# The input projection of groups 2 to 4 moved into the first scan, with the gate's matmul reading x contiguously

## Chip, cores and metric

The kernel runs on one core of a Trainium2 chip. The metric is device time in microseconds (us) of one execution; the figure before is the median of three runs. A profile of one further execution shows every engine: TensorE (PE, with its weight loads PEld), VectorE (DVE), ScalarE (ACT), GpSimd (POOL) and SyncE (SP, which issues most DMAs).

## The reference

Input x is 32 sequences of 256 tokens of 256 features, all float32. The result is x plus an FFN block applied to a conditioning block:

```
x + ffn(cond(x, cond_2048))

cond:  xr, gate = split(x @ W_in.T)            # 256 -> 2 x 512
       xr  = silu(causal conv of 4 taps (xr + cond_2048))
       xn  = layernorm(xr)
       B, C, dt = split(xn @ W_xproj.T)        # 16 states each
       h_t = clip(h_(t-1) * a_t + b_t x xn_t, -10, 10)     # 256 steps
       y_t = C_t . h_t + D * xn_t
       out = (y * silu(gate)) @ W_out.T
ffn:   two layers of local attention (8 heads, windows of 128)
       and a gated feed-forward (hidden 682), each with a residual
```

## The kernel before

The sequences are taken in four groups of eight (GB = 8). For each group there is a scan (the conditioning block) and a main part (two layers of attention and feed-forward, `blocks`). The scan of group 1 (`g == 0` in the code, `alone`) runs by itself at the start. Then the main part of each group is issued with the scan of the next group beside it: `side_by_side` takes the pieces of both generators in proportion, so each engine's queue has the two interleaved. The main part of group 4 has no scan beside it.

A scan puts 16 states by 8 sequences on the 128 partitions and the 512 inner features along the free dimension. It goes in chunks of 32 tokens (CH), eight per group, and is written as an agenda: `at(s, what, ...)` puts a piece of work at step s, and step s of the recurrence is also piece s. With s0 the first step of a chunk, the parts that matter here are:

- `load_x` (line 340) at s0 - 43: SP issues two DMAs of 128 KB into `xg` (two buffers).
- `project` (line 322): one block of 128 output rows of the input projection, two matmuls of 128 x 256 that accumulate, each of which the profile shows as two records. The four conv blocks stand at s0 - 40, -38, -36 and -34, the four gate blocks at s0 + 13, 16, 17 and 18. The gate blocks read x with its tokens in another order, since the gate is needed in the order in which the scan's results are laid out:

```
if ch >= NC_:
    x = x.rearrange("p b (i q) -> p q i b", q=NQ)
```

- `conv_in` (line 351), `conv_taps`, `conv_out` take a conv block out of its PSUM bank, and lead to the normalised `xn`, which is written to memory as `xnd` (line 462) and read back spread over the states as `xrep` (line 547; three buffers of two tokens each).
- `scale_row` (line 564, ACT) scales a row, `step` (line 570, DVE; profile line 573) is the recurrence, `read_out` (line 580, PE; line 585) forms y from four steps at a time with four matmuls.
- `gate_th` (line 617, ACT) and `gate_out` (line 622, DVE) turn a gate block into `sg`, one and two steps after its projection.
- `raw_sums` (line 393), `norm_turn` (line 418), `figures` (line 474), `out_turn` (line 634) and `project_y` (line 658) are the scan's other matmuls.

In the first scan, half of the rows are spread by PE instead of DMA (`spread_rows`, line 549, into `bx`, from `xq`, which `load_skip` loads into the `rot` buffers). PSUM is one pool of eight banks with one tag, `w`, for everything. Each engine works through its own queue in the order in which the program was built.

## Time and profile before

| | us |
|---|---|
| median of three runs | 4182.01 (4180.69 to 4185.67) |
| the profiled execution | 4183.47 |
| its span, first to last instruction | 4181.7 |
| mean granted TensorE clock | 0.966 of full |
| first scan, step 0 to step 255 | 70.7 to 462.8 |
| last additions of groups 1, 2, 3, 4 | 1502.3, 2492.6, 3486.8, 4175.4 |

The profile's page gives busy time of each engine over the span, then in 40 equal slices. Views by stage give, for a stretch of time, its length and each engine's busy time with the number of records, then the granted PE clock, the share of time in which the DMA engines were busy, and GB/s. Lists in order of time give the start, the time that the merged run of records takes, the engine, the line, what is written from what, and, in brackets, the idle time before it and who ended it. Lists of groups give after the bar the busy time, the mean ns of one record, and the idle time ahead of it with who ended most of it. Matmuls overlap in the pipeline and their ends are modelled, so a matmul's own time is longer than the time from its start to the next one's start.

### The profile page before, as it was taken

To read this page: it belongs to the slowest core of one execution; us is meant where nothing else is said; L and a number is where in the kernel's file an instruction comes from. 1 tells how busy PE (TensorE), PEld (TensorE's weight loads), DVE (VectorE), ACT (ScalarE), POOL (GpSimd) and SP (SyncE) were. 2 spreads that over 40 slices of the span, in tenths; PEclk is the share of its full clock that TensorE was granted. 3 is DMA by queue.
4 is the path that set the end of the run, shared out by engine and by line. 5 is a ranking of instruction groups with operands and counts; after the bars stand their busy time and mean duration, and the time that the engine had idled before them with its cause. 6 is when DMAs were issued, how large, how long until landed. Compare 5 with 4: busy or idle time off the path is not lost. (4 is left out here: it accounts for less than half of the span.)

```text
span 4181.7 us, 51837 instructions
## 1 busy us (share of the span) xinstructions
PE 3874.3 (93%) x18236; PEld 2002.1 (48%) x18236; DVE 2619.7 (63%) x4986; ACT 1742.8 (42%) x3217; POOL 1708.1 (41%) x1749
## 2 busy tenths in 40 slices
PE   6999899899988999899998999989998899999999
PEld 3333355444544455444455445544454545654653
DVE  5888467677766456766867636776776644434443
ACT  2555344444444334444544424444444533322331
POOL 3443265225543156423654136522454315513531
PEclk9999899999999999999999999999999999999999
DMA  3444213444335212344434421344433521000000
GB/s 123 121 124 119 58 44 95 113 117 112 91 87 139 81 43 77 111 110 111 116 86 114 121 65 44 81 126 111 118 91 84 142 78 37 3 19 22 1 11 31
DMA packets 257345, 353.09 MB, mean 84 GB/s; under 512 B 160867, under 2 KB 170420, under 8 KB 254900
## 3 DMA queue, kind: packets, MB, share of 16 engines
q1 hardware_dynamic: 172624, 337.67, 29.0%
q10 hardware_dynamic: 84452, 12.01, 1.8%
q8 instruction: 147, 2.41, 0.2%
q14 instruction: 122, 1.00, 0.1%
HBM read 314.49 MB, written 33.55 MB: 83 GB/s over the span
## 5 line engine op out<-in xcount | busy, mean ns | idle before, releaser
L573 DVE CUSTOM_DVE_ANT_0 h<-h,xrep,lim 128x512 f32<-128x512 f32 x1024 | 908.1, 887 | 94.8 <-PE y L585 36.0
L566 ACT ACTIVATE xrep<-xrep,beta 128x512 f32<-128x512 f32 x896 | 608.6, 716 | 793.3 <-DMA xrep<-xnd 732.8
L781 PE MATMUL ps_qkv<-wqkv_sb,res 128*128 128x512 f32 x1536 | 740.5, 621 | 28.4 <-ACT qT L825 6.6
L805 POOL TENSOR_TENSOR rot<-rot,swp 128x512 f32<-128x512 f32 x256 | 329.2, 1286 | 653.3 <-DVE swp L802 603.3
L781 PEld LDWEIGHTS ps_qkv<-wqkv_sb,res 128*128 128x128 f32 x1536 | 286.6, 196 | 381.9 <-issue 309.0
L813 POOL TENSOR_TENSOR rn<-ss,neg_half 128x8 f32<-128x8 f32 x256 | 437.4, 1708 | 21.6 <-DVE ss L811 9.7
L797 DVE TENSOR_TENSOR rot<-ps_qkv,rc_sb 128x512 f32<-128x512 f32 x256 | 175.6, 686 | 375.6 <-ACT sq L794 375.4
L330 PE MATMUL ps_in<-xg,w_in_sb 128*128 128x256 f32 x1024 | 398.4, 523 | 6.5 <-ACT pT L995 3.4
L1140 PE MATMUL po_f<-ag,w_sb 128*128 128x512 f32 (+1 forms) x768 | 356.0, 612 | 18.5 <-DVE ag L1121 18.5
L585 PE MATMUL y<-h,ly 128*32 128x512 f32 x2048 | 354.0, 639 | 11.3 <-DVE h L573 10.1
L1111 PE MATMUL pa<-hT,w_sb 128*128 128x512 f32 (+1 forms) x896 | 363.0, 595 | 0.0
L1121 DVE SCALAR_TENSOR_TENSOR ag<-pa,b_sb,gl 128x512 f32<-128x512 f32 x192 | 143.5, 747 | 317.9 <-PE pa L1111 166.2
L1111 PE MATMUL pg<-hT,w_sb 128*128 128x512 f32 x640 | 309.4, 606 | 0.0
L330 PEld LDWEIGHTS ps_in<-xg,w_in_sb 128*128 128x128 f32 x1024 | 194.1, 204 | 206.5 <-issue 125.2
L814 POOL TENSOR_TENSOR rot<-rot,rn 128x512 f32<-128x512 f32 x256 | 280.3, 1095 | 19.0
L377 DVE SCALAR_TENSOR_TENSOR acc<-xr,wc_sb,acc 128x256 f32<-128x256 f32 x384 | 199.2, 523 | 116.7 <-POOL acc L366 114.2
L1074 POOL TENSOR_TENSOR rstd<-ve,neg_half 128x1 f32<-128x1 f32 x128 | 75.8, 592 | 476.6 <-DVE ve L1072 466.1
L995 ACT ACTIVATE pT<-sc 128x512 f32<-128x512 f32 x384 | 206.3, 592 | 127.3 <-PE sc L986 113.7
L831 PE MATMUL ps_wo<-oT,wo_sb 128*128 128x256 f32 x1024 | 237.3, 385 | 0.0
L1140 PEld LDWEIGHTS po_f<-ag,w_sb 128*128 128x128 f32 (+1 forms) x768 | 135.1, 190 | 203.3 <-issue 138.7
L794 ACT ACTIVATE sq<-ps_qkv 128x512 f32<-128x512 f32 x256 | 148.8, 593 | 195.9 <-PE ps_qkv L781 148.1
L1111 PEld LDWEIGHTS pa<-hT,w_sb 128*128 128x128 f32 (+1 forms) x896 | 135.6, 170 | 189.3 <-issue 175.7
(151 smaller groups left out, 5592.9 us busy)
## 6 DMA issues: line engine op xcount, KB each, us to landing
xrep<-xnd SPq DMA_DIRECT2D x448, 512.0 KB
xnd<-xn SPq DMA_DIRECT2D x64, 256.0 KB
wqkv_sb<-in_wqkv_dram SPq DMA_DIRECT2D x8, 1536.0 KB
xd<-xnd SPq DMA_DIRECT2D x192, 64.0 KB
w_sb<-in_w_dram SPq DMA_DIRECT2D x8, 1364.0 KB
xg<-in_xT_dram SPq DMA_DIRECT2D x64, 128.0 KB
ys<-yo ACTq DMA_DIRECT2D x64, 128.0 KB
res<-ys SPq DMA_DIRECT2D x32, 256.0 KB
```

What stands on the lines that cost most here:

```text
L330: nc.tensor.matmul(ps, w_in_sb[:, k, ch * P : (ch + 1) * P], x, start=(k == 0), stop=(k == KM - 1),)
L566: nc.scalar.activation(bx, ck[c].pop(("bx", t), bx), AF.Copy, scale=ck[c]["beta"][:, t : t + 1])
L573: nc.vector._custom_dve(TENSOR_ADD_SAT, out=h_new, in0=state["h"], in1=bx, s0=ck[c]["lim"][:, 0, t : t + 1], s1=ck[c]["lim"][:, 1, t : t + 1],
L585: nc.tensor.matmul(ck[c]["y", hb][32 * q : 32 * q + 32, :], ly[hb % 2][:, 32 * t : 32 * t + 32], ck[c].pop(("h", hb * TB + t)), start=(i = ...
L781: nc.tensor.matmul(ps, res[b // 2][:, k, b % 2, t0 : t0 + W], wqkv_sb[:, k, a * DI : (a + 1) * DI], start=(k == 0), stop=(k == KM - 1),)
L805: nc.gpsimd.tensor_add(rot, rot, swp)
L813: nc.gpsimd.tensor_tensor(rn, ss, neg_half, ALU.pow)
L814: nc.gpsimd.tensor_mul(rot, rot, bc(rn, 2, DH))
L831: nc.tensor.matmul(po[:, d], wo_sb[:, c, d * P : (d + 1) * P], oT[:, c, :], start=(c == 0), stop=(c == NC_ - 1),)
L995: nc.scalar.activation(p, banks[r], AF.Exp)
L1111: nc.tensor.matmul(ps[0:n, :], self.w1[:, k, half_ * HID + o : half_ * HID + o + n], self.h[j][:, k].rearrange("p b t -> p (b t)"), start= ...
L1140: nc.tensor.matmul(self.po[d], self.w2[r0 : r0 + n, m, d * P : (d + 1) * P], self.ag[m][r0 : r0 + n, :], start=(m == 0), stop=(m == len(MC ...
```

## The change

The scan of group 1 now also makes the input projection of groups 2 to 4. There are 96 units, each of two blocks (r = 0, 1) of one chunk of one group: 3 groups x 8 chunks x 4 pairs. For unit u, due at step s = -36 + u * 284 // 96, the program adds a load of x for every fourth unit (at s - 5), four matmuls into one PSUM bank (at s), a copy by ACT to SBUF (at s + 2) and a DMA of 256 KB to a buffer in memory (at s + 5). The scans of groups 2 to 4 no longer load x or project; they load 256 KB with two finished blocks, four times per chunk, at s0 - 44, s0 - 42, s0 + 3 and s0 + 5, and the blocks are read from SBUF where they were read from PSUM.

All projections, those of group 1's own gate too, now read x contiguously. The gate's tokens are put in their other order by ACT when it copies from PSUM (`reorder`): for the 48 gate units in two halves each, and for group 1's own gate block by block into `sg`, which `gate_th` and `gate_out` then read.

The new loads of x take buffers of tag `rot`, the copies buffers of tag `pT` (six, one of them held by the spreading weights in this scan); the loads of finished blocks take the two of tag `xg`. Nothing else of the computation is changed.

```diff
+        def reorder(out, ps):
+            nc.scalar.copy(
+                out.rearrange("p (q i b) -> p b i q", q=NQ, b=GB),
+                ps.rearrange("p (b i q) -> p b i q", q=NQ, b=GB),
+            )
+
+        projected = {}
...
-            def project(c, ch):
-                ps = bank(ps_w, "w", "ps_in")[:, 0 : GB * CH]
+            def in_rows(ps, xg, ch):
                 for k in range(KM):
-                    x = ck[c]["xg"][:, k]
-                    if ch >= NC_:
-                        x = x.rearrange("p b (i q) -> p q i b", q=NQ)
                     nc.tensor.matmul(
                         ps,
                         w_in_sb[:, k, ch * P : (ch + 1) * P],
-                        x,
+                        xg[:, k],
                         start=(k == 0),
                         stop=(k == KM - 1),
                     )
+
+            def project(c, ch):
+                ps = bank(ps_w, "w", "ps_in")[:, 0 : GB * CH]
+                in_rows(ps, ck[c]["xg"], ch)
                 ck[c]["ps", ch] = ps
+
+            def ahead_load(u):
+                if u % NC_ == 0:
+                    gg, c = 1 + u // NC_ // NCH, u // NC_ % NCH
+                    t = ap_.tile([P, KM, GB, CH], FP, tag="rot", name="xa", bufs=4)
+                    for k in range(KM):
+                        nc.sync.dma_start(
+                            out=t[:, k],
+                            in_=xT[:, k, gg * GB : (gg + 1) * GB, c * CH : (c + 1) * CH],
+                        )
+                    state["xa", u // NC_] = t
+
+            def ahead_project(u):
+                ps = bank(ps_w, "w", "ps_a").rearrange("p (r n) -> p r n", r=2)
+                for r in range(2):
+                    in_rows(ps[:, r], state["xa", u // NC_], 2 * (u % NC_) + r)
+                state["pa", u] = ps
+
+            def ahead_copy(u):
+                t = aw.tile([P, 2, GB * CH], FP, tag="pT", name="xs_a", bufs=6)
+                ps = state.pop(("pa", u))
+                if u % NC_ < NC_ // 2:
+                    nc.scalar.copy(t, ps)
+                else:
+                    for r in range(2):
+                        reorder(t[:, r], ps[:, r])
+                state["ta", u] = t
+
+            def ahead_put(u):
+                d = dp.tile([P, 2, GB * CH], FP, tag=f"ahead{u}", name=f"ahead{u}", bufs=1)
+                nc.sync.dma_start(out=d, in_=state.pop(("ta", u)))
+                projected[u] = d
+
+            def load_projected(c, i):
+                t = sp.tile([P, 2, GB * CH], FP, tag="xg", name="xp", bufs=2)
+                nc.sync.dma_start(out=t, in_=projected[((g - 1) * NCH + c) * NC_ + i])
+                for r in range(2):
+                    ck[c]["ps", 2 * i + r] = t[:, r]
...
             def gate_th(c, ch):
-                th = sp.tile([P, GB * CH], FP, tag="th", name="th_g", bufs=2)
-                nc.scalar.activation(th, ck[c]["ps", NC_ + ch], AF.Tanh, scale=0.5)
-                ck[c]["th"] = th
-
-            def gate_out(c, ch):
                 if ch == 0:
                     ck[c]["sg"] = sp.tile([P, NC_, GB * CH], FP, tag="sg", name="sg")
+                ps = ck[c].pop(("ps", NC_ + ch))
+                if alone:
+                    reorder(ck[c]["sg"][:, ch], ps)
+                    ps = ck[c]["sg"][:, ch]
+                th = sp.tile([P, GB * CH], FP, tag="th", name="th_g", bufs=2)
+                nc.scalar.activation(th, ps, AF.Tanh, scale=0.5)
+                ck[c]["th"] = th, ps
+
+            def gate_out(c, ch):
+                th, ps = ck[c].pop("th")
                 nc.vector.scalar_tensor_tensor(
-                    ck[c]["sg"][:, ch], ck[c].pop("th"), 1.0, ck[c].pop(("ps", NC_ + ch)),
-                    ALU.add, ALU.mult,
+                    ck[c]["sg"][:, ch], th, 1.0, ps, ALU.add, ALU.mult
                 )
...
-                at(s0 - 43, load_x, c)
-                for ch in range(NC_):
-                    at(s0 - 40 + 2 * ch, project, c, ch)
-                for ch, s in enumerate((13, 16, 17, 18)):
-                    at(s0 + s, project, c, NC_ + ch)
+                if alone:
+                    at(s0 - 43, load_x, c)
+                    for ch in range(NC_):
+                        at(s0 - 40 + 2 * ch, project, c, ch)
+                    for ch, s in enumerate((13, 16, 17, 18)):
+                        at(s0 + s, project, c, NC_ + ch)
+                else:
+                    for i, s in enumerate((-44, -42, 3, 5)):
+                        at(s0 + s, load_projected, c, i)
...
+            if alone:
+                n = (NG - 1) * NCH * NC_
+                for u in range(n):
+                    s = -36 + u * (NCH * CH + 28) // n
+                    at(s - 5, ahead_load, u)
+                    at(s, ahead_project, u)
+                    at(s + 2, ahead_copy, u)
+                    at(s + 5, ahead_put, u)
```

## The prediction

> **What bounds the kernel now.** I read the totals first, then stages. On the page, in the engine rows and the 40 slices, TensorE (PE) is the only engine near full:

> ```profile
> PE 3874.3 (93%) x18236; PEld 2002.1 (48%) x18236; DVE 2619.7 (63%) x4986; ACT 1742.8 (42%) x3217; POOL 1708.1 (41%) x1749
> ...
> PE   6999899899988999899998999989998899999999
> ```

> The starts of the recurrence steps (line 573) and the last additions of a group (line 1164) give stage borders: the first scan, alone, runs from 70.7 to 462.8 us; group 2's blocks with a scan beside them from 1502.3 to 2492.6; group 4's blocks, with none, from 3486.8 to 4175.4. The last row is six chunks of the first scan. Busy time by stage:

> ```profile
> core 0: us, PE busy (x) PEld busy (x) DVE busy (x) ACT busy (x) POOL busy (x), PEclk, DMA share, GB/s
> 70.70:462.80 392.10, 370.57 (x1297) 128.76 (x1294) 328.46 (x599) 211.40 (x384) 142.74 (x169) 0.93 0.44 115
> 1502.30:2492.60 990.30, 925.11 (x4480) 489.45 (x4480) 653.94 (x1233) 433.30 (x804) 423.27 (x434) 0.97 0.36 97
> ...
> 3486.80:4175.40 688.60, 673.03 (x3320) 371.00 (x3320) 291.61 (x564) 218.36 (x394) 262.09 (x221) 0.99 0.04 13
> 125.00:411.60 286.60, 269.11 (x1007) 100.10 (x1006) 253.92 (x476) 161.56 (x296) 117.70 (x138) 0.96 0.47 122
> ```

> A stage with a scan is 990.3 - 688.6 = 302 us longer than one without, and PE is 252 us busier; no other engine reaches 67%. So beside a scan, PE work is paid nearly in full. The same view of line 330 (the input projection) alone:

> ```profile
> 70.70:462.80 392.10, 92.65 (x224) 42.65 (x224) 0.93 0.44 115
> 1502.30:2492.60 990.30, 98.10 (x256) 47.78 (x256) 0.97 0.36 97
> ```

> Some 98 us of each scan's PE time, with the modelled tails of the matmuls, is this projection. The first scan looks as full (370.57 of 392.10 busy), but that is not work. PE's order of time, from three stretches of it:

> ```profile
> 68.18 1.99 PE L330 MATMUL ps_in<-xg,w_in_sb 128*128 128x256 f32 x8
> 70.11 1.98 PE L555 MATMUL bx<-xq,rep_w 32*128 32x512 f32 x7
> ```
> ```profile
> 151.01 3.81 PE L330 MATMUL ps_in<-xg,w_in_sb 128*128 128x256 f32 x8
> 154.75 1.13 PE L555 MATMUL bx<-xq,rep_w 32*128 32x512 f32 x4
> ...
> 161.05 1.13 PE L330 MATMUL ps_in<-xg,w_in_sb 128*128 128x256 f32 x4
> 162.11 1.06 PE L585 MATMUL y<-h,ly 128*32 128x512 f32 x8
> 163.11 1.13 PE L330 MATMUL ps_in<-xg,w_in_sb 128*128 128x256 f32 x4
> ```
> ```profile
> 324.37 4.34 PE L585 MATMUL y<-h,ly 128*32 128x512 f32 x8 [0.61 <-DVE h L573]
> 328.64 0.65 PE L638 MATMUL tz<-ident,xd 128*128 128x128 f32 x4
> ```

> From one start to the next: a row block of the projection with contiguous x holds PE 162.11 - 161.05 = 1.06 us, a pair of them 1.93; a pair of gate blocks, which read x strided, 3.74, so 1.87 each. Eight y records take 1.00 us when their steps are ready and 4.27 when PE follows VectorE (DVE) step by step: the first scan has hidden room.

> [...] about 510 y records are busy 138.3 us in the first scan and 70.8 in group 2's. [...] The gate's read steps 32 floats between elements; it costs 1.87 against 1.06. [...] PEclk is 0.93 in the first scan and 0.99 where PE is fed, so filling gaps should not slow PE. [...]

> **The change part by part.**

> (a) *Taken out of three scans.* Each had 8 chunks with 4 conv blocks at 1.06 and 4 gate blocks at 1.87: 8 x (4.24 + 7.48) = 93.8 us, three scans 281 us. A little work fills waits there: PE stands idle 65.2 us in 990.3 with a scan and 15.6 in 688.6 without, so I count 90%: **-253 us**. If every block lay on the path it is -281; if a quarter refilled with waits, -211.

> (b) *The first scan's gate reads contiguously*: per chunk 7.48 becomes at most 4.24, -3.3 us of PE. Its price is four ACT copies with a strided write and 4 tanh from SBUF.

> (c) *Put into the first scan*: 96 units of 4 matmuls (8 records), two contiguous blocks each, 1.93 us per unit, 185 us of PE. They are spaced 2.96 steps from step -36, so 12 stand before step 0 and 84 in the scan: 10.5 x 1.93 = 20.3 us per chunk. A chunk asks PE now for 7.48 + 4.24 (projection) + 8 x 1.05 (bx) + 8 x 1.00 (y) + about 8.8 (raw sums, output projection, turns, figures) = 36.9 us, and takes 286.6/6 = 47.8. Afterwards: 36.9 - 3.3 + 20.3 = 53.9. DVE keeps 253.92/6 = 42.3 and no longer decides. For waits I add 3.4, near the 17.5/6 = 2.9 us idle now: 57.3 us per chunk. Eight times (57.3 - 47.8) = **+76 us**. With no waits (49 us) to 65 us per chunk (138 us) are the ends.

> (d) *ACT in the first scan*: 48 plain copies and 96 + 32 copies with strided writes. Nearest rows, of group 2's stage and of the first scan:

> ```profile
> L825 ACT COPY qT<-tr_qk 128x512 f32<-128x512 f32 x32 | 18.7, 585 | 9.1 <-PE tr_qk L820 9.0
> ```
> ```profile
> L672 ACT COPY yo<-ps_out 128x256 f32<-128x256 f32 x14 | 8.4, 603 | 12.2 <-PE ps_out L661 9.6 <-ACT yo L672 2.7
> ```

> 48 x 0.585 + 128 x 0.603 = 105 us. ACT, 211 us busy now, comes to some 316 of 460: it hides beside PE. If it doesn't, PE waits for banks, the rival below.

> (e) *SyncE (SP) and the DMAs*. The first scan gets 48 loads of 128 KB and 96 stores of 256 KB, some 0.56 us of SP each as its issues show, 81 us on a queue that mostly waits; later scans lose 48 loads and gain 96 of 256 KB. The first scan moves 115 GB/s at a share of 0.44; the added 31 MB over 460 us are 68 GB/s, so the share comes to about 0.63 and hides. A store waits for its copy, and xrep loads (line 547), xq and xnd queue behind it; ACT's next scaling waits for these. The copy is due three steps earlier, so I take zero; -0 to +20 us.

> (f) *Before step 0*: PE is idle most of 52 to 63 us, but four units (7.7 us) are issued ahead of the raw sums, two more around the turns, and stores and weights stand ahead of xnd on SP. **+7 us**, 0 to 15.

> (g) *Later scans*: loads into two buffers at steps -44, -42, 3, 5 replace those at -43. Gate reads end two steps before the buffer is wanted again. A late one would hold xrep behind it. I take zero; 0 to +20. conv_in and gate_out read SBUF instead of PSUM on DVE, 66% busy: nothing either way. Eight banks get freer: no gain counted.

> Sum: -253 + 76 + 7 = **-170 us**. The profiled execution took 4183.5 us (span 4181.7, 1.8 around it), the median is 1.5 less: 4183.5 - 170 = **4013**.

> **The rivals.**

> *First scan coupled to ACT, mild* (0.12). A unit's bank is freed by an ACT copy queued behind scalings that wait for DVE and DMA (43.7 us for xrep in this scan). For: PE already waits there for ACT releases. Against: ACT would be under 70% busy. At 66 us per chunk: -253 + 146 + 7, 4083.

> *The same lockstep, severe: slower* (0.04). Each unit stalls PE until ACT has copied an earlier one. From 78.6 us per chunk on, (253 - 7)/8 = 30.8 above now, all is lost; at 85 us: -253 + 298 + 7, 4235. It needs 2.4 us of stall for each of the 84 units; the copies are due two steps later, which speaks against it.

> *Waits take the place* (0.06). Half of (a) was cover for chains such as DVE swp to scores: -127 + 83, 4140. Against: the 302 us against 252 above.

> *More than forecast* (0.12): all 281 us, a first scan at 54.5: -281 + 54 + 4, 3960.

> *The matmuls don't sit in the first scan* (0.01): the program as built has all 384 between its steps, so only a late end could do it; 4180.

> **How the numbers follow.** The forecast has 0.65, with 3970 to 4060 of its own. The range to the mild rival and the better case: 3960 to 4085. A measurement here tells 0.2%, some 8 us, from no change. Faster 0.94, same 0.02, slower 0.04.

> **What would show it.** Right: stages with a scan near 900 us with PE under 840 busy; first scan 440 to 480 with y at about 1 us per eight; ACT there under 75%. Wrong: PE waiting for ACT copies at line 334 by over 50 us, xrep waits for DMA growing by tens of us, or idle PE in later stages rising above 90 us each.

## The result, and the profile after

Over five runs of each, the kernel after takes 4160.33 us (4154.49 to 4164.93) and the kernel before 4182.01 (4179.05 to 4186.25): a ratio of 0.9947, with a 95% interval of 0.9934 to 0.996. That is 22 us gained where 170 were forecast, and outside the range given. The direction was right; seven eighths of the gain are missing.

The page of the kernel after, engine totals and the PE row of the 40 slices:

```profile
PE 3755.8 (90%) x18236; PEld 2011.8 (48%) x18236; DVE 2631.9 (63%) x4986; ACT 1828.1 (44%) x3393; POOL 1719.0 (41%) x1749
...
PE   7889889789888999889988899979988899999999
```

PE is busy 118 us less than before with the same number of matmuls, and yet the kernel is only 22 us faster: look for PE standing idle. The 9s of the middle slices have become 8s. By stage, with borders read as before (a stage ends here with the end of a group's last addition):

```profile
75.50:548.20 472.70, 427.80 (x1968) 248.93 (x1967) 348.79 (x617) 290.16 (x546) 135.74 (x180) 0.93 0.60 156
548.20:1549.70 1001.50, 886.32 (x4294) 459.63 (x4293) 666.65 (x1266) 438.80 (x816) 448.95 (x450) 0.94 0.39 105
1549.70:2511.50 961.80, 859.33 (x4224) 445.87 (x4224) 653.43 (x1233) 432.32 (x805) 430.42 (x432) 0.94 0.39 106
...
3470.20:4158.10 687.90, 671.01 (x3316) 369.20 (x3315) 291.24 (x564) 218.27 (x394) 262.30 (x220) 0.99 0.04 13
```

Columns are the window, its length, busy time of PE, PEld, DVE, ACT and POOL, the granted PE clock, the DMA share and GB/s. In group 2's stage PE is busy 66 us less than before (859.3 against 925.1), but the stage is only 28.5 us shorter (961.8 against 990.3). PE idle went from 65 to 102 us, and the granted clock from 0.97 to 0.94. Laid out over the borders of the two profiled executions, in us:

| | before | after | difference | forecast |
|---|---|---|---|---|
| before step 0 | 70.7 | 75.5 | +4.8 | +7 |
| first scan | 392.0 | 472.6 | +80.6 | +76 |
| group 1's stage | 1040.9 | 1001.5 | -39.4 | |
| group 2's stage | 990.3 | 961.8 | -28.5 | |
| group 3's stage | 994.2 | 958.7 | -35.5 | |
| the three together | | | -103.4 | -253 |
| group 4's stage, no scan | 688.7 | 687.9 | -0.8 | 0 |

The first scan did what was expected, as far as one profile of each tells: in three other runs below the same first scan as before, with the same sequence on DVE, took 379.7, 386.4 and 387.5 us, so the 80.6 could as well have been 93. PE's order of time in it:

```profile
318.91 1.89 PE L334 MATMUL ps_a<-xa,w_in_sb 128*128 128x256 f32 x8
320.73 1.13 PE L605 MATMUL bx<-xq,rep_w 32*128 32x512 f32 x4
321.79 1.06 PE L635 MATMUL y<-h,ly 128*32 128x512 f32 x8
322.78 1.99 PE L334 MATMUL ps_a<-xa,w_in_sb 128*128 128x256 f32 x8
```

A unit of two blocks holds PE 1.82 us (320.73 - 318.91), and eight y records take 0.99 (322.78 - 321.79) and no longer 4.27. Over the whole scan y is busy 77.4 us instead of 138.8: PE has all but stopped following DVE. The rest is in the stages with a scan, and the experiments go there.

### The profile page after: what moved, and what is told of

It reads as the page before. It is cut to its first block, busy times and chain, and to the rows that moved or that the text cites. A ratio compares the mean times of both kernels' runs of the same rounds, so it can differ in the third digit from the quotient of the medians.

```text
span 4163.0 us, 52386 instructions
## 1 busy us (share of the span) xinstructions
PE 3755.8 (90%) x18236; PEld 2011.8 (48%) x18236; DVE 2631.9 (63%) x4986; ACT 1828.1 (44%) x3393; POOL 1719.0 (41%) x1749
## 5 line engine op out<-in xcount | busy, mean ns | idle before, releaser
L623 DVE CUSTOM_DVE_ANT_0 h<-h,xrep,lim 128x512 f32<-128x512 f32 x1024 | 924.4, 903 | 114.1 <-ACT xrep L616 48.4
L847 PE MATMUL ps_qkv<-wqkv_sb,res 128*128 128x512 f32 x1536 | 750.6, 629 | 43.8 <-ACT oT L1097 11.9
L879 POOL TENSOR_TENSOR rn<-ss,neg_half 128x8 f32<-128x8 f32 x256 | 448.3, 1751 | 41.4 <-DVE ss L877 33.5
L1206 PE MATMUL po_f<-ag,w_sb 128*128 128x512 f32 (+1 forms) x768 | 366.9, 628 | 28.7 <-DVE ag L1187 28.6
L1177 PE MATMUL pg<-hT,w_sb 128*128 128x512 f32 x640 | 319.2, 622 | 0.0
L635 PE MATMUL y<-h,ly 128*32 128x512 f32 x2048 | 298.9, 625 | 14.1 <-DVE h L623 8.7
L1140 POOL TENSOR_TENSOR rstd<-ve,neg_half 128x1 f32<-128x1 f32 x128 | 78.6, 616 | 543.7 <-DVE ve L1138 480.6
L1052 PE MATMUL sc<-qT,kT 64*128 64x128 f32 (+1 forms) x2048 | 226.4, 351 | 1.5 <-ACT kT L891 1.1
L897 PEld LDWEIGHTS ps_wo<-oT,wo_sb 128*128 128x128 f32 x1024 | 189.9, 190 | 45.5 <-issue 19.3
```

The source lines that it names most:

```text
L623: nc.vector._custom_dve(TENSOR_ADD_SAT, out=h_new, in0=state["h"], in1=bx, s0=ck[c]["lim"][:, 0, t : t + 1], s1=ck[c]["lim"][:, 1, t : t + 1],
L635: nc.tensor.matmul(ck[c]["y", hb][32 * q : 32 * q + 32, :], ly[hb % 2][:, 32 * t : 32 * t + 32], ck[c].pop(("h", hb * TB + t)), start=(i = ...
L847: nc.tensor.matmul(ps, res[b // 2][:, k, b % 2, t0 : t0 + W], wqkv_sb[:, k, a * DI : (a + 1) * DI], start=(k == 0), stop=(k == KM - 1),)
L879: nc.gpsimd.tensor_tensor(rn, ss, neg_half, ALU.pow)
L897: nc.tensor.matmul(po[:, d], wo_sb[:, c, d * P : (d + 1) * P], oT[:, c, :], start=(c == 0), stop=(c == NC_ - 1),)
L1052: nc.tensor.matmul(banks[r][:, i, :], kT[rows, i0 + i, kw * W : (kw + 1) * W], qT[rows, i0 + i, kw * W :], start=False, stop=(i == n - 1),)
```

## The experiments

Theories at the outset. **M**: the projection's matmuls filled time in which PE would have waited anyway, so removing them leaves waits. **L**: what the change puts in their place (loads, reads from SBUF, ACT's reordering) costs time. **K**: the longer waits make PE run at half clock, and that eats the gain (the granted clock of group 2's stage fell from 0.97 to 0.94). A fourth, **X**, blames the DMA that brings `xrep`. The expectations also speak of W, which is M under another name, and of P, which comes up with the shift of the agenda. All totals are medians, and each ratio is to runs of the kernel before taken beside it, whose medians lie between 4177.7 and 4181.3 us. Stage times are from one profile each, so a difference of a few us in one stage is weak evidence by itself.

### Pure removal, and the new loads left out

In `e1_none` the kernel before leaves out the loads of x and the projection in the scans of groups 2 to 4; conv and gate read a constant. In `e2_noload` the kernel after leaves out the loads of finished blocks and reads a constant.

```diff
 e1_none
-                    at(s0 - 40 + 2 * ch, project, c, ch)
+                    at(s0 - 40 + 2 * ch, project if alone else given, c, ch)
...
-                    at(s0 + s, project, c, NC_ + ch)
+                    at(s0 + s, project if alone else given, c, NC_ + ch)
 e2_noload
-                t = sp.tile([P, 2, GB * CH], FP, tag="xg", name="xp", bufs=2)
-                nc.sync.dma_start(out=t, in_=projected[((g - 1) * NCH + c) * NC_ + i])
...
-                    ck[c]["ps", 2 * i + r] = t[:, r]
+                    ck[c]["ps", 2 * i + r] = blk
```

> The kernel before, with the projection left out of the scans of groups 2 to 4: no x loads and no projection matmuls there, conv_in and the gate read a fixed piece of SBUF instead, so those groups' values are not the reference's. It is term (a) alone. Theory W (the projection stood in waits of PE, little of it was on the path): each stage with a scan falls by 30 to 40 us, the total by 90 to 120, about 4075. Theory L (PE was the bound, and the new loads of finished blocks hold up the SP queue and eat the gain): each stage falls by 80 to 94, the total by 240 to 280, about 3920.

> The changed kernel, with the loads of finished blocks left out of the scans of groups 2 to 4 (they read a fixed piece of SBUF, so those groups' values are not the reference's); the first scan is unchanged. Theory W: within 10 us of the changed kernel, 4150 to 4165. Theory L: the stages with a scan fall to about 905 us each, the total to about 4000.

`e1_none`: 4041.2 us, ratio 0.9671 [0.9655, 0.9688]. The three stages are 983.9, 948.3 and 942.9: 57, 42 and 51 us shorter, 150 in all, where 281 us of PE time were taken out by the prediction's count and nothing was put in. That is more than theory W's 30 to 40 a stage and far less than the 80 to 94 of full payment. So about half of the projection's time does not come back even with nothing of the change's own cost. `e2_noload`: 4161.3, the kernel after again; the loads cost nothing that shows, which speaks against L. But the kernel after falls 47 us short of `e1_none` in these stages, and that part needed another reason.

### Putting the matmuls back, and the gate's reading alone

`e3_idle` is the kernel after with the projection's matmuls issued again in the later scans, at their old steps, on weights instead of x and with nobody reading the result. `e4_gate` is the kernel before with nothing moved: the gate's matmul reads contiguously and ACT reorders. `e7_gates` moves only the gate's blocks into the first scan (48 units) and leaves the conv blocks where they were.

```diff
 e3_idle
...
+                    for ch in range(NC_):
+                        at(s0 - 40 + 2 * ch, idle_rows, ch)
+                    for ch, s in enumerate((13, 16, 17, 18)):
+                        at(s0 + s, idle_rows, NC_ + ch)
 e4_gate
-                    if ch >= NC_:
-                        x = x.rearrange("p b (i q) -> p q i b", q=NQ)
...
+                nc.scalar.copy(
+                    ck[c]["sg"][:, ch].rearrange("p (q i b) -> p b i q", q=NQ, b=GB),
+                    ps.rearrange("p (b i q) -> p b i q", q=NQ, b=GB),
+                )
...
```

> The changed kernel, with as many projection matmuls as before put back on PE at the old steps of the scans of groups 2 to 4, on fixed data, the gate's with the strided read; nobody reads their results. It prices that PE work in its place. Theory W: the stages go back to about 990 us, +90 to +110 in total, 4260, a third of the work's 281 us; PE's half-clock time and idle time in these stages go back to those of before. If PE were the bound in the changed kernel's stages: +240 to +280, about 4420.

> The kernel before with the second part of the change alone: the gate's matmul reads x contiguously in all four scans, ACT puts the tokens in order when it copies from PSUM. PE is freed of 0.81 us x 32 blocks = 26 us per scan. Theory W: the first scan has room anyway (0 to -15 us), the stages give about a third of 26 each, the total falls by 15 to 40, about 4155. Were PE the bound in the stages: -26 each, the total down by 80 to 95. If the longer chain through ACT decides, slower by 10 to 30.

> Half of the move: only the gate blocks of groups 2 to 4 (48 units) are made in the first scan; their conv blocks stay where they were, with the x loads at step -43. Nothing is left out. PE is asked for 36.9 - 3.3 + 48/96 x 20.3 = 43.7 us per chunk of the first scan, under the 47.8 that it takes: +5 to +25 us there. The later stages lose 60 of 94 us of PE work; at half of that, -30 each. Theory W with a cheap first scan: total down 65 to 85, about 4105. If the first scan pays for every unit (+40) and the stages give a fifth: 4180, no gain.

`e3_idle`: 4337.9, ratio 1.0385 [1.0367, 1.0402], where theory W had 4260. Its stages are 1058.6, 1016.9 and 1014.0. Putting some 98 us of matmuls back into each costs 57, 55 and 55. But they are also 18 to 27 us longer than those of the kernel before, which does the same matmuls: something else in the change holds the stages back. `e4_gate`: 4160.5, ratio 0.9953 [0.9939, 0.9967]; stages 11, 7 and 8 us shorter for some 26 us of PE time each (8 chunks x 4 blocks x 0.81), a first scan 8 us longer. `e7_gates`: 4146.0, ratio 0.9926 [0.991, 0.9943]; stages 24, 20 and 19 us shorter for 60 us of gate blocks each (8 x 7.48), a first scan 23 us longer; the total fell by 35 us where 65 to 85 were expected. In each variant between a quarter and six tenths of what is removed comes off the stage.

### One piece of the agenda

What else holds the stages back lies in how the agenda is dealt out. A scan's generator gives one piece for each step from the lowest step in its agenda, and `side_by_side` deals pieces out in proportion. The kernel before starts at s0 - 43. The change puts its first load at s0 - 44, and so moves every piece of the scan by one against the main part. `e6_shift` is the kernel after with that load one step later. `e8_shift_before` gives the kernel before an empty piece at s0 - 44.

```diff
 e6_shift
-                    for i, s in enumerate((-44, -42, 3, 5)):
+                    for i, s in enumerate((-43, -42, 3, 5)):
 e8_shift_before
+                if not alone:
+                    at(s0 - 44, lambda: None)
```

> The changed kernel with the first load of each chunk at step -43 instead of -44, so that the later scans' agendas begin at -43 as before, and every scan piece meets the piece of the main part that it met before; nothing is left out. Theory P (the added step moved the whole scan by one piece against the main part, which made some of the waits): stages fall by 10 to 25 us each, the total by 30 to 70, about 4110. Theory W (waits as in any order): within 10 us of the changed kernel, 4160.

> The kernel before with an empty piece at step -44 in the scans of groups 2 to 4 and nothing else: no instruction is added or taken, the scan moves by one piece against the main part. Theory P: stages grow by 10 to 25 us each, the total by 30 to 70, about 4230. Theory W: within 10 us of before, 4180.

`e6_shift`: 4116.2, ratio 0.9856 [0.9837, 0.9875], 44 us faster than the kernel after for one digit. `e8_shift_before`: 4196.3, ratio 1.0037 [1.0025, 1.0048], 15 us slower for an empty step, which is less than the 30 to 70 of theory P. `e6_shift` also issues one load a step later, but that is not the cause: `e2_noload` has no loads at all, keeps the agenda that starts at s0 - 44, and is as slow as the kernel after. Group 2's stage in `e6_shift`, and then PE's wait for the normalised row `hn` in the same stage of the kernel before, the kernel after and `e6_shift` (in this order):

```profile
1537.30:2478.50 941.20, 849.25 (x4226) 443.15 (x4225) 656.93 (x1233) 432.89 (x805) 432.32 (x432) 0.95 0.40 108
```

```profile
L1089 PE MATMUL tp_hn<-ident,hn 128*128 128x128 f32 x64 | 12.9, 284 | 16.8 <-DVE ve L1072 11.7 <-DVE hn L1076 5.1
```

```profile
L1155 PE MATMUL tp_hn<-ident,hn 128*128 128x128 f32 x64 | 13.6, 297 | 29.0 <-DVE hn L1142 18.9 <-DVE ve L1138 10.1
```

```profile
L1155 PE MATMUL tp_hn<-ident,hn 128*128 128x128 f32 x64 | 13.4, 294 | 33.2 <-DVE hn L1142 19.7 <-DVE ve L1138 13.6
```

The stages are now 988.7, 941.2 and 940.2: within some 7 us of `e1_none`, which has no loads of blocks, no reordering and no projection. So in the old pairing loads, SBUF reads and reordering cost nothing that shows, and **L is refuted** there; undoing the shift takes 13, 21 and 18 us off the stages. In the shifted pairing L is not ruled out: `e3_idle` and `e8_shift_before` have the same matmuls at the same steps, and the stages of `e3_idle`, which takes its blocks from memory, are 14, 14 and 15 us longer. The `hn` waits, which grew from 16.8 to 29.0 us, stand at 33.2 in `e6_shift` and at 28.9 in `e1_none`: they belong to the removal, not to the shift.

`e12_idle43` closes the books: `e6_shift` with the matmuls put back as in `e3_idle`.

> The one-piece-shifted version of the change (loads at steps -43, -42, 3 and 5) with the projection's matmuls put back on PE in the scans of groups 2 to 4 at their old steps, the gate's strided; their result is not read. It does the projection twice, so its only difference from the kernel before in the later stages is where the blocks come from and which engine reads them. If loads, SBUF reads and the gate's reordering cost nothing and the books close, stages 2 and 3 stand at 985 to 1000 us as before, that is 45 to 55 us above the shifted version although some 94 us of matmuls come back per stage, and the total is the time before plus the first scan's 80 to 90, about 4265. If each matmul is paid in full, stages are 1035 or more and the total about 4400. If something else in the change holds the stages back, they stand above 1010 with PE idle above 85.

Its median is 4265.4, ratio 1.0205 [1.0187, 1.0223]; the forecast was about 4265. Group 2's and group 3's stages, all engines, then the returned matmuls alone (PE and PEld):

```profile
1581.50:2570.10 988.60, 920.37 (x4482) 488.59 (x4482) 659.00 (x1233) 435.86 (x805) 423.81 (x432) 0.97 0.38 103
2570.10:3566.10 996.00, 926.34 (x4482) 489.74 (x4481) 646.12 (x1202) 434.02 (x801) 415.95 (x410) 0.96 0.37 101
```

```profile
1581.50:2570.10 988.60, 99.10 (x256) 49.35 (x256) 0.97 0.38 103
2570.10:3566.10 996.00, 98.48 (x256) 48.60 (x256) 0.96 0.37 101
```

988.6 and 996.0 are the stages of the kernel before (990.3 and 994.2). The two programs `e6_shift` and `e12_idle43` differ in these matmuls and their PSUM banks alone, so here the price of the projection beside a scan can be read. Mean of the two stages: 98.8 us of matmul records cost 51.6 us of stage (988.6 - 941.2 and 996.0 - 940.2).

Records overlap, so the 98.8 holds tails that are counted twice. If each matmul is counted from its start to the next one's start, or to the end of its record where PE then waits, the two stages divide like this (means, in us; a remainder of 1 us lies at the borders):

| | `e6_shift` | `e12_idle43` | difference |
|---|---|---|---|
| the projection's matmuls | 0 | 90 | +90 |
| all other matmuls | 849 | 832 | -17 |
| PE idle | 91 | 69 | -22 |
| stage | 941 | 992 | +52 |

So 90 us of matmuls are paid with 52: 22 us of them fill time in which PE would stand idle, and the *other* matmuls take 17 us less. Of those others' time, 67 us ran at half clock in `e6_shift` and 40 in `e12_idle43`. If a matmul takes twice as long there, that makes 14 of the 17 us (an estimate; eight y records take 1.93 us at half clock below, and 1.06 at full). **This is the missing part of step (a).**

### The half clock

The clock records of the trace show 62 us at half clock in group 2's stage before, 108 after, 88 in `e6_shift`, 67 in `e12_idle43`. One such place in the kernel after, as three windows one after another:

```profile
1706.40:1713.20 6.80, 4.03 (x30) 2.33 (x30) 5.86 (x14) 4.84 (x11) 3.25 (x6) 1.00 0.69 200
1713.20:1716.60 3.40, 3.01 (x10) 1.38 (x7) 3.24 (x9) 2.49 (x6) 2.98 (x3) 0.50 0.23 63
1716.60:1720.00 3.40, 3.40 (x9) 1.52 (x8) 3.40 (x6) 1.23 (x3) 3.40 (x3) 1.00 0.01 2
```

In 6.8 us PE is busy 4.03, its longest wait being 1.90 us; then it runs 3.4 us at clock 0.50. If the one follows from the other, a wait is paid twice. To see whether that half clock is what eats the gain (K), `e10_warm` puts five unread matmuls (4.46 us at 1760.23 in its trace) ahead of the first transpose of `hn` where the waits are longest, and `e13_warm2` as many as fill the waits (8, 11 and 4).

```diff
 e10_warm, against e6_shift (in spread)
+                if j == 0 and (self.l, n) in ((0, 0), (0, 2), (1, 0)) and self.g < NG - 1:
+                    for _ in range(5):
+                        nc.tensor.matmul(
+                            tp, w_in_sb[:, 0, 0:P], w_in_sb[:, 0, 0:DI], start=True, stop=True
+                        )
```

> e6_shift with work added on PE: five matmuls of 128 x 512 (about 4.3 us at full clock) whose result is overwritten, just ahead of three transposes per stage (line 1155) at which PE always waits 5 to 11 us and after which its clock is halved for 7 to 14 us. Theory K (a wait is paid twice, the second time at half clock): half-clock time falls by 15 us or more per stage and the total by 20 to 45 although PE does more, about 4085. If the clock after the wait costs nothing: 4116, or up to 20 more where the filler outlasts the wait.

> The shifted version with unread filler matmuls ahead of the first transpose of hn, in a number that fills the wait for hn (8 in the first layer's spread(0, 0), 11 in its spread(0, 2), 4 in the second layer's spread(0, 0)), in the stages with a scan beside. If it is the half clock after the waits that eats the gain, half-clock time falls by some 25 us per stage and the total by 20 to 40 against the shifted version (4116). If it is the waits themselves, nothing is gained: total the same to 20 us longer, and PE idle falls by about what is put in.

`e10_warm`: 4130.6, ratio 0.9884 [0.9869, 0.9899], 14 us slower than `e6_shift`. `e13_warm2`: 4133.5, ratio 0.9883 [0.9865, 0.99], 17 slower. Its group 2 stage has PE busy 26 us more and idle 14 less than `e6_shift`, and is 12 us longer; the half-clock time is 93 us instead of 88. Over the three stages with a scan half-clock time falls from 298 us to 286 and 275, where the expectations wanted 45 and 75 less. **K is not confirmed as the whole answer**, nor refuted: the fillers hardly brought the half clock down, and in `e10_warm` PE still waited 3.6 and 7.4 us behind two of them. What sizes K is the table above, up to 14 of the 38 us that go missing in a stage.

### Who holds PE in the long waits

PE's order of time in `e6_shift` at one of the long waits:

```profile
1752.67 0.41 PE L1130 MATMUL tp_h<-ident,res 128*128 128x128 f32 x2 [2.81 <-DVE swp L868]
1761.10 0.66 PE L1155 MATMUL tp_hn<-ident,hn 128*128 128x128 f32 x2 [8.02 <-DVE hn L1142]
1761.69 1.93 PE L635 MATMUL y<-h,ly 128*32 128x512 f32 x8
```

and DVE's order of time beside it:

```profile
1758.12 0.68 DVE L905 TENSOR_TENSOR res<-res,ps_wo 128x512 f32<-128x512 f32 x1
1758.72 0.76 DVE L1134 BATCH_NORM_STATS2 st<-tp_h 128x6 f32<-128x256 f32 x2
...
1760.41 1.06 DVE L1142 TENSOR_SCALAR hn<-tp_h,mv,rstd 128x256 f32<-128x256 f32 x2 [0.53 <-POOL rstd L1140]
```

`tp_h` is done at 1753, but DVE takes its statistics only at 1758.72, after three steps of the scan (line 623, 2.93 us from 1755.28) and an addition to the residual; `hn` comes at 1760.41. DVE is busy 70% of the whole stage (656.93 of 941.20), but 7.30 of the 7.90 us from 1753.2 to 1761.1: here it is the bound, and PE waits. PE then does eight y records in 1.93 us instead of 1.06, at half clock. The granted clock is 0.62 in the wait from 1753.2 to 1761.1 and 0.56 from there to 1766.0, so here the half clock begins within the wait and not only after it, as the expectation of `e10_warm` has it.

If that chain were the missing half, giving it other cover would return it. `e14_later` issues `spread(0, n)`, which holds these transposes, one slot later on PE. `e16_later_before` does the same to the kernel before.

```diff
                     at.turn(b, 1)
+                    if b == GB - 1:
+                        ff.spread(0, 1)
...
-                        ff.spread(0, 2 * (b - GB + 2))
...
-                        ff.spread(0, 2 * (b - GB + 2) + 1)
+                        ff.spread(0, 2 * (b - GB + 2))
...
                 at.divide(GB - 1)
+                ff.spread(0, 3)
```

> The shifted version with the transposes of hn and the products that follow, spread(0, n) of the feed-forward, issued one slot later on PE in each of the two layers, so that hn's chain over DVE and POOL has other PE work beside it. If the lost half is this chain's fixed time of about 8 us, PE's waits for hn (about 33 us per stage) fall by half or more, each stage with a scan by some 15 to 30 us and the total by 50 to 90 against the shifted version. If the waits only move to the products after it, to the gate's turn or to the scan's DVE, the stages stay within 8 us and the total within 20.

> The kernel before with spread(0, n) issued one slot later, as in the run above with the moved projection. If the projection's matmuls covered part of hn's chain, the waits for hn here are only some 17 us per stage instead of 33, so the later issue brings less than the 9 us per stage that it brought there: 0 to 5 us in each stage with a scan, and 15 us in the last stage, which has no projection in either kernel: 15 to 30 us in all, about 4157. If the later issue's gain has nothing to do with the projection, it is the same 40 us, about 4140.

Group 2's `hn` group in `e14_later`, and then in `e16_later_before`:

```profile
L1155 PE MATMUL tp_hn<-ident,hn 128*128 128x128 f32 x64 | 13.1, 288 | 13.2 <-DVE ve L1138 8.3 <-DVE hn L1142 4.8
```

```profile
L1089 PE MATMUL tp_hn<-ident,hn 128*128 128x128 f32 x64 | 12.5, 277 | 1.9 <-DVE hn L1076 1.2 <-DVE ve L1072 0.7
```

`e14_later`: 4076.0, ratio 0.9747 [0.973, 0.9763], 40 us under `e6_shift`, below the 50 to 90 that the theory wanted. The `hn` waits fell by 20 us in this stage, the stage by 9: more than half of what was freed went into other waits. 15 of the 40 us come from group 4's stage (688.7 to 673.8), which has no scan. `e16_later_before`: 4143.7, ratio 0.9915 [0.9893, 0.9938], 36 us under the kernel before, nearer to the 40 of the rival reading than to 15 to 30; in group 2's stage 15 us of waits went and the stage fell by 4 (990.3 to 986.5). The moved and aligned projection is worth 65 us without the later issue (4181.3 to 4116.2) and 68 with it (4143.7 to 4076.0), the same within the noise. So the two gains add, and **the chain to `hn` is not where the projection's gain went**, though it is the largest single wait. Against `e12_idle43`, PE's waits in group 2's stage of `e6_shift` are longer by 9.5 us for `hn`, 6.4 for `rs`, 5.1 for `ps_qkv`, 4.7 for `sc` and 3.0 for `po_f`: M holds for 22 us a stage, as cover for many short waits and not for one chain.

### The xrep transfers

`e5_noxrep` and `e9_noxrep_before` leave out the loads of `xrep` in the scans of groups 2 to 4, from the kernels after and before; the rows scaled there are a constant. `e11_xp4` is `e6_shift` with four buffers for them instead of three (and six for `hp` instead of eight, to make room). `e15_best` adds the later issue to it.

```diff
 e5_noxrep, e9_noxrep_before
-                if not by_tensor(t):
+                if alone and not by_tensor(t):
...
 e11_xp4, e15_best
-        hp = ctx.enter_context(tc.tile_pool(name="hp", bufs=8, reuse_waits="tile"))
-        xp = ctx.enter_context(tc.tile_pool(name="xp", bufs=3, reuse_waits="tile"))
+        hp = ctx.enter_context(tc.tile_pool(name="hp", bufs=6, reuse_waits="tile"))
+        xp = ctx.enter_context(tc.tile_pool(name="xp", bufs=4, reuse_waits="tile"))
```

> The changed kernel, with the xrep loads left out of the scans of groups 2 to 4: scale_row reads a constant there, so those groups' values are not the reference's; every other instruction stays. Theory X (the waits that took the projection's place come from the scan's xrep loads: ACT's scalings wait for them, DVE's steps wait for ACT, and the main part's small DVE and ACT work queues behind): PE's idle time per stage falls from about 100 to 50 us or less and the stages to 900 or less, the total to about 4000 or below. Theory M (the waits belong to the main part's own chains through DVE, POOL and ACT): stages stay within 15 us, the total within 45 of 4160.

> The control of e5_noxrep: the kernel before with the same xrep loads left out of the scans of groups 2 to 4 and a constant read there, so those groups' values are not the reference's. Theory X (with the xrep waits gone PE is the bound in the stages, and the projection's PE work is paid nearly in full): stages near 980 us, 75 to 95 above e5_noxrep's 903.5 and 898.7; the total 4140 to 4170. Theory M (the loads slow both kernels alike, and the projection is worth no more without them): stages near 940, 30 to 45 above; total about 4040.

> e6_shift with four xrep buffers instead of three, and six h buffers instead of eight to make room; nothing is left out. Theory X by way of the buffers (a load can start only when a step frees its buffer, so it arrives late): ACT's waits for xrep in the stages fall by a third or more, stages by 10 to 25 us, the total to about 4065. If the load's own time or the order decides: within 10 us of e6_shift. If six h buffers are too few, DVE's steps wait for y: slower by 10 to 40.

> The same later issue of spread(0, n) on the shifted version with four buffers for xrep and six for hp. If the two gains add, it is 13 us under the run above; if the buffers' gain came from the same waits, the two agree within 6 us.

Group 2's stage without the loads, kernel after and then kernel before:

```profile
1504.30:2407.80 903.50, 833.86 (x4226) 439.50 (x4226) 657.24 (x1233) 433.58 (x805) 431.77 (x432) 0.97 0.13 39
```

```profile
1441.10:2391.30 950.20, 910.86 (x4480) 485.11 (x4479) 648.48 (x1233) 433.04 (x805) 420.90 (x433) 0.98 0.11 30
```

`e5_noxrep`: 3997.0, ratio 0.9561 [0.9544, 0.9578]; `e9_noxrep_before`: 4039.8, ratio 0.9671 [0.9656, 0.9686]. By itself `e5_noxrep` looked like theory X (stages of 903.5 and 898.7 us, and a total near 4000); its control came out as theory M had it (950.2 and 4039.8 for 940 and 4040). The transfers cost both kernels: group 2's stage 58 us after, 40 before. Without them the change takes 47 us off this stage (950.2 to 903.5) instead of 28.5, shift included. But of some 90 us removed, half is still missing with no `xrep` to wait for: X explains a part at most. `e11_xp4`: 4103.3, ratio 0.9825 [0.9812, 0.9839], 13 us under `e6_shift`; by its profile 9 us of it lie in the first scan, 9 in group 1's stage and none in groups 2 and 3's beyond 2 us, and ACT's wait for the transfers is 645 us in the whole kernel instead of 651, not less by a third. The buffers help the first scan and do not cure X. `e15_best`: **4062.9 us, ratio 0.9716 [0.97, 0.9732]**, the fastest version that computes the whole result, 13 us under `e14_later` as expected of gains that add.

## Why the prediction was wrong

**What bounds the kernel** was read too generally. "Beside a scan, PE work is paid nearly in full" came from 302 us of stage against 252 of PE busy. That is the *mean* price of a whole scan, with the scan's waits in it. What the change needed was the *marginal* price of taking one part out of an interleaved stage, and this is 52 us for 90 (`e12_idle43` against `e6_shift`).

**(a), "so I count 90%: -253 us", is the step that failed.** The 65.2 us of idle PE were read as a measure of how much work fills waits. They say what is left uncovered, not what would be uncovered next. What took the place of the 10% is measured: of 90 us taken out of a stage, 22 came back as PE idle and 17 as longer times of the other matmuls, 14 of it from the half clock by the estimate above, a term that (a) does not have. (The work itself was 90 us a stage rather than 93.8, which matters little.) Aligned, the three stages fell by 155 us (52 + 49 + 54), 55% of 281; `e1_none`, with nothing put in, gives 150. As the change was made they fell by 103, since the shift gave 52 of it back by these profiles (44 by the medians of the totals). Even the end of the range, -211 with "a quarter refilled with waits", was too high.

**(g), "I take zero; 0 to +20",** looked at late loads. Those cost nothing that shows (`e2_noload`). What cost 52 us was that one of them was numbered a step earlier than anything before it, and moved the whole scan by a piece. The step is in the text (-44, against -43); that the lowest step of the agenda sets the pairing with the main part was not thought of.

**(b)** took nothing separate for the later stages, since (a) included it; `e4_gate` gives 7 to 11 us a stage for it. The gate's tanh, which reads SBUF in the kernel after, took 413 ns in the first scan, for 382 from PSUM before. **(c)**, +76, was +80.6; the waits added were 27 us for the scan where PE's idle time is 44.9, of which 38.4 are seven waits of the statistics matmul `ps_st` for DVE, 10.4 before. That the difference fits is in part luck: the scan took 472.6 us for 8 x 57.3 = 458, and the scan before 392.0 for 8 x 47.8 = 382. **(d)** was right: the copies take 102 us for the forecast 105, and ACT is busy 290 of 473 us, 61%. **(e)** was right on the DMA share, 0.60 for 0.63, but ACT's waits for `xrep` in this scan grew from 43.7 to 101.7 us. How much of PE's waits there goes back to them is not shown; with four `xrep` buffers this scan is 9 us shorter (`e11_xp4`). **(f)**, +7, was +4.8.

**The rivals.** Coupling to ACT did not come, in either strength: PE waited 1.1 us for ACT at line 334. "Waits take the place", half of (a) and 4140, had much of the mechanism. Its 4140 lies between the 4160.3 that was measured and the 4116.2 without the shift, which it did not have. The chain it named, swp to scores, hardly shows: PE's waits at `sc` grew by 0.1 and 2.6 us from the kernel before to `e6_shift` (groups 2 and 3). It was given 0.06 on the strength of the 302 against 252. Of the signs named beforehand for being wrong, idle PE above 90 us in each later stage is what the trace shows (115, 102 and 97), and the `xrep` waits grew by tens of us, in the first scan.

**The clock.** The prediction took it that filling gaps should not slow PE, and in the first scan the clock did stay at 0.93. The converse was not considered: in group 2's stage, where PE idles 102 us for 65, the trace shows 108 us at half clock for 62. Ahead of the half clock in the windows at 1706 the longest wait is 1.90 us.

**What stays open.** The 38 us that go missing in a stage without the shift are split into 22 of idle PE and 17 of slower other matmuls. That the half clock makes most of the 17 is an estimate; no run holds the clock and changes the waits. No single wait carries the 22: in `e6_shift` the `hn` waits are 33 of 92 us of idle time, and freeing 20 of them gave 9. One piece of shift costs 15 us in the kernel before, 44 in the kernel after, and 72 with the matmuls put back (`e3_idle` against `e12_idle43`). Which waits the shift makes, and why its price depends on the rest, was not followed further.

## What to carry to other kernels

The price of removing work from a stage where several queues are interleaved need not be its busy time, however full the engine looks (here 52 us for 90, in stages where PE is busy 93% of the time): put the same work back unread, or leave it out with nothing in its place, and read the marginal price before building the move. When work is dropped from a hand-written interleaving, keep every other piece at its old place, since moving the pairing by one step cost twice what the change gained (44 us for 22). And where an engine's idle time grows, list its waits before trusting the largest: here a wait that was cut by 20 us gave back 9.

## What the runs showed of the hardware that was not expected

The time at half clock also differs between profiles of the same work. The first scan of the kernel before, with one sequence on DVE in four runs, had 17 us at half clock where it took 379.7 us (`e9_noxrep_before`), 34 at 386.4 (`e16_later_before`), 41 at 387.5 (`e8_shift_before`) and 51 at 392.0: about a third of a us for each us at half clock.
